# A state-space scan on one core: zero products on TensorE, a later sum, one more C buffer and |x| in place

## The chip, the core and the metric

The kernel runs on one core of a Trainium2 chip, in one launch. A core has five engines that run their own instruction queues in order: TensorE (matrix products, PE in the profile, with its weight loads as PEld), VectorE (DVE), ScalarE (ACT), GpSimd (POOL) and SyncE (SP), which here only issues DMAs. They meet through semaphores. TensorE writes to PSUM; the other operands lie in SBUF. The metric is device microseconds (us) of one execution: before the change 568.95, 570.45 and 570.57, so a median of 570.45 us.

## The reference, cut to what matters

Two layers run one after the other on a 64 x 64 image of 96 channels, all in float32. The change touches only the second, a Mamba layer over the sequence of L = 4096 pixels, with 192 inner channels and 16 states:

```
xs, z = split(gn(x) @ W_in.T);  xc = silu(causal_conv3(xs))
dt, B, C = split(xc @ W_x.T);   delta = softplus(dt @ W_dt.T + b_dt)
h[t] = exp(delta[t] * A) * h[t-1] + delta[t] * B[t] * xc[t]     # for each channel and state
y[t] = sum over states of h[t] * C[t]  + xc[t] * D
out = x + (y * silu(z)) @ W_out.T
```

## The kernel before, in words

**Tiles.** The sequence is cut into four chunks of 1024 steps (`NSC`, `CH`). The 192 channels are one full tile of 128 partitions and a half tile of 64. In a chunk the scan has 24 *units* (`UNITS`, `UNIT`): units 0 to 15 are one state each of the full tile, units 16 to 23 are two states each of the half tile, one state on either half of the partitions. So 96 units follow each other; s counts them, and `c, i = divmod(s, 24)` gives the chunk and the place in it. Data of the half tile are 512 columns wide per half (the columns `CH:CW` of a tile of `CW` = 1536), and are spread to the form of units 16 to 23 by DMAs (`front_dup`).

**One unit.** `load` (L1492) brings C[t] of the state, the same row on all partitions, by DMA from DRAM into a buffer of the pool `"C"`, which has six; `decay` (L1502) makes exp(delta*A) on ScalarE; `spread` (L1511) puts B[t] on all partitions of a PSUM tile `f` by two bf16 products (f has two buffers); `scan` (L1525) multiplies f by w = delta*xc on VectorE and runs the recurrence there into `h` (three buffers); `times_c` (L1544) multiplies the C buffer by h on GpSimd; `fold` (L1560) adds that product to the sum over states with two float32 matrix products, into `y0` (two banks, units 0 to 15) or `y1` (one bank, units 16 to 23). At i = 0 `fold` first calls `skip` (L1548), which starts the sum with xc*D. In five units of a chunk (`POOL_UNITS`, L42) B comes by DMA too, GpSimd multiplies it by w (`pool_f`), and the decay lies in an f buffer instead.

**The order.** Everything goes through the class `Ordered`, whose helper at L377 records each instruction and makes it follow the one before it on its engine; so nearly all rows of the profile have line L377, and the order is the order of the calls in `run` (L1804). Its loop does for each s, in this order: the next step of the *work between* (`all_between`); `load(s+3)`; `spread(s+1)` if that unit isn't one of GpSimd's; `keep_last(s-1)` (ScalarE saves the last column of h); the decays of the units ahead, and `pool_f`; the next step of `soft`; `scan(s)`; `times_c(s-1)`; `fold(s-2)`; and at i = 20 `gate(c, 0)` (L1579), where VectorE multiplies the finished y0 by silu(z).

**The work between** (`between`, L1738) prepares the next chunk and finishes the last one on TensorE and ScalarE, a step per unit, with at most two calls of a product in it, all through one PSUM bank `misc`. Names of its products in the profile: pc (convolution), pd (projection to dt, B, C), pv (delta before the softplus), pz (z), po (the output), pt (transposes of it). In chunks 1 and 2 the steps i = 2 and 3 are pd; at i = 4 VectorE gates y1 of the chunk before (`gate(c - 1, 1)`), and TensorE then starts the new y1 with `skip(c, 2)` and goes on to pv. In chunk 3 there is no pd, and this gate with its `skip` comes at i = 3, followed by po. In chunk 1 the last pc is copied by ScalarE at i = 14, and po follows in the same step; in chunk 2, po is copied at i = 12 before pt.

**The softplus** (`soft`, L1770) of the next chunk is spread over the units as well: from i = 15 in chunk 0 and from i = 10 in the others, one step per unit: |x| on ScalarE into a tile `e`; two sigmoids of e into `acc` and `q`; the first square of q; the second; `soft_times` on VectorE; the last VectorE operation, into dt; w = dt*u on GpSimd; the DMAs. In the opening chunk a part of it runs at i = 2 and after.

**What the steps of the prediction touch:** the functions named above, and the PSUM and SBUF buffers that make one engine wait for another: f (released by the scan), C (released by the fold, so SyncE's loads wait for TensorE), h (released by `times_c`, so a scan waits for GpSimd's third product before it), `misc` (released by a ScalarE copy).

Of the kernel before, what the change touches and what calls it, by code (L numbers as in the profile page):

```python
# [20 lines left out]
C = 96  # L21
DI = 192
NS = 16
# [14 lines left out]
UNIT = len(UNITS[0]) + len(UNITS[1])  # L38

WHOLE = 4  # L40

POOL_UNITS = ((5, 11, 15, 19, 23), (4, 8, 12, 16, 21), (4, 8, 12, 16, 21), (4, 8, 12, 16, 20))  # L42
CW = CH + NB
# [171 lines left out]
def soft_scalar(nc, k, e, last, q):  # L215

    soft_logistic(nc, k, e, last, q)
    for i in range(2):
        soft_square(nc, k, q, i)
# [1050 lines left out]
class Layer1:  # L1270
# [6 lines left out]
    def __init__(self, nc, tc, st, k, lay, w_in, conv_w, x1, stats, bc_dram, out, g):  # L1277
        self.k, self.lay, self.x1, self.bc_dram, self.out = k, lay, x1, bc_dram, out
        self.g = g
        self.pools = {  # L1280
            n: st.enter_context(tc.tile_pool(name=f"{n}_1{g}", bufs=b))
            for n, b in (
                ("fix", 1), ("xn", 2), ("uz", 2), ("sp", 1), ("dt", 2), ("dup", 2), ("dbl", 1),
                ("parts", 2), ("split", 1), ("B", 1), ("C", 6), ("dA", 3), ("h", 3), ("v", 1), ("oc", 1),
                ("ob", 2),
            )
        }
        fix = self.pools["fix"]
        self.cw = tap_weights(nc, fix, w_in, conv_w, 3, f"1{g}")
        self.nc = nc = Ordered(nc, tc)  # L1290
        with tc.tile_pool(name=f"gn1{g}", bufs=1, space=PSUM) as ps:

            warm = ps.tile([P, NB], F32, name=f"warm{g}")

            def busy(n, cols=NB):
                for _ in range(n):
                    nc.tensor.matmul(
                        warm[:, 0:cols], k["ident"][0:C, :], x1[:, 0:cols], start=True, stop=True
                    )

            busy(2)
            self.mean, self.rstd = group_norm_scale(
                nc, fix, ps, k["grp"], stats, f"1{g}", lambda: busy(1, NB // 2)
            )
            busy(2)
        self.shift = fix.tile([C, 1], F32, name=f"shift1{g}")
        nc.vector.scalar_tensor_tensor(
            self.shift, self.mean, -1.0, self.rstd, ALU.mult, ALU.mult
        )

        self.diag = fix.tile([P, 2, P], F32, name=f"diag{g}")
        for t in range(2):
            nc.gpsimd.tensor_scalar(
                self.diag[:, t, :], k["ident"], lay["vec"][:, DSK + t : DSK + t + 1], None, ALU.mult
            )
        self.last = fix.tile([P, UNIT], F32, name=f"last{g}")
        for n, b in (("f", 2), ("y0", 1), ("y1", 1), ("misc", 1)):
            self.pools[n] = st.enter_context(
                tc.tile_pool(name=f"{n}_1{g}", bufs=b, space=PSUM)
            )  # L1320
# [105 lines left out]
    def front_v(self, c):  # L1426
        nc, of = self.nc, self.chunks[c]
        self.at = c
        of["e"], of["dt"] = e, dt = self.tile("sp", [P, CW], "e"), self.tile("dt", [P, CW], "dt")
        of["acc"], of["q"] = self.tile("sp", [P, CW], "acc"), self.tile("sp", [P, CW], "q")  # L1430
        for q in range(3):
            ps = self.misc(c, [P, NB], f"pv{q}")
            yield from self.steps(self.product(ps, q, self.dt_taps(of["dbl"])))
            nc.scalar.activation(dt[:, self.part(q)], ps, AF.Identity, bias=self.vec(DTB, q))
# [141 lines left out]
                )  # L1576


    def gate(self, c, t):  # L1579
        of, col = self.chunks[c], (slice(0, CH), slice(CH, CW))[t]  # L1580
        self.at = c
        if t == 0:
            of["v"] = self.tile("v", [P, CW], "v")
        self.nc.vector.tensor_mul(of["v"][:, col], of[f"y{t}"], of["sz"][:, col])
# [70 lines left out]
    def start(self):  # L1655

        nc, of = self.nc, self.chunks[0]
        self.at = 0
        xn = of["xn"] = self.tile("xn", [C, CH + 2], "xn")
        nc.gpsimd.memset(xn[:, 0:2], 0.0)  # L1660
        nc.vector.tensor_scalar(
            xn[:, 2 : 2 + NB], self.x1[:, 0:NB], self.mean, self.rstd, ALU.subtract, ALU.mult
        )
        nc.scalar.activation(
            xn[:, 2 + NB :], self.x1[:, NB:CH], AF.Identity, scale=self.rstd, bias=self.shift
        )

        table = lambda func: nc.scalar.activation(self.k["root"], self.k["ones"], func)
        table(AF.Silu)
        self.front_xn(1)  # L1670
        self.at = 0
        u = of["u"] = self.tile("uz", [P, CW], "u")
        dbl = of["dbl"] = self.tile("dbl", [ROWS, CH], "dbl")
        e, acc, sq = of["e"], of["acc"], of["q"] = [
            self.tile("sp", [P, CW], n) for n in ("e", "acc", "q")
        ]
        dt = of["dt"] = self.tile("dt", [P, CW], "dt")

        def do(matmuls):
            for args, kw in matmuls:  # L1680
                nc.tensor.matmul(*args, **kw)

        def bank(pool, shape, name):
            self.at = name
            return self.tile(pool, shape, pool)

        pc = [bank("f", [P, NB], f"pc{p}") for p in range(2)] + [self.misc(0, [P, NB], "pc2")]
        pd = [bank(f"y{hf}", [ROWS, NB], f"pd{hf}") for hf in range(2)]

        for p in range(3):  # L1690
            do(self.product(pc[p], p, self.conv_taps(xn)))
            nc.scalar.activation(u[:, self.part(p)], pc[p], AF.Silu, bias=self.vec(CB, p))
        table(AF.Sigmoid)
        for hf in range(2):
            do(self.project(0, hf, pd[hf]))
            nc.vector.tensor_copy(dbl[:, self.part(hf)], pd[hf])
            self.write_bc(0, hf)
        pv = [bank("f", [P, NB], f"pv{p}") for p in range(2)] + [self.misc(0, [P, NB], "pv2")]
        for p in range(3):
            do(self.product(pv[p], p, self.dt_taps(dbl)))  # L1700
        for p in range(2):
            col = self.part(p)
            nc.scalar.activation(e[:, col], pv[p], AF.Abs, bias=self.vec(DTB, p))
            soft_scalar(nc, self.k, e[:, col], acc[:, col], sq[:, col])
            nc.vector.tensor_scalar(dt[:, col], pv[p], self.vec(DTB, p), 0.0, ALU.add, ALU.max)
        for s in range(3):
            self.load(s)
        for p in range(2):
            col = self.part(p)
            soft_vector(nc, dt[:, col], acc[:, col], sq[:, col])  # L1710
        self.front_w(0, (slice(0, CH),), nc.vector)
        self.spread(0)
        self.spread(1)

        pz, pz1 = bank("y0", [P, 2, NB], "pz"), bank("y1", [P, NB], "pz1")
        for q in range(2):
            do(self.product(pz[:, q], q, self.z_taps(xn)))
        do(self.product(pz1, 2, self.z_taps(xn)))
        for s in range(2):
            self.decay(s)  # L1720
        nc.scalar.activation(dt[:, self.part(2)], pv[2], AF.Identity, bias=self.vec(DTB, 2))
        for _ in self.front_b(0, halves=True):
            pass
        self.at = 0
        sz = of["sz"] = self.tile("uz", [P, CW], "sz")
        for q in range(3):
            nc.scalar.copy(sz[:, self.part(q)], pz[:, q] if q < 2 else pz1)
# [42 lines left out]
    def soft(self, c):  # L1770

        def piece(c, col):

            nc, k = self.nc, self.k
            e, dt, acc, q = (self.chunks[c][n][:, col] for n in ("e", "dt", "acc", "q"))
            nc.scalar.activation(e, dt, AF.Abs)
            yield
            soft_logistic(nc, k, e, acc, q)
            yield
            for i in range(2):  # L1780
                soft_square(nc, k, q, i)
                yield
            soft_times(nc, acc, q)
            yield
            nc.vector.scalar_tensor_tensor(dt, dt, 0.0, acc, ALU.max, ALU.add)
            yield
            self.front_w(c, (col,), nc.gpsimd)
            yield
            self.front_dup(c)
            yield  # L1790
# [13 lines left out]
    def run(self):  # L1804
# [2 lines left out]
        self.units = [{} for _ in range(n)]  # L1807
        self.start()
        work, end = self.all_between(), self.end()
        for s in range(n + 2):  # L1810
            c, i = divmod(s, UNIT)
            if i == 0 and c < NSC:
                soft = self.soft(c)
# [19 lines left out]
                self.times_c(s - 1)  # L1833
            if s == n:
                next(end)
            if s >= 2:
                self.fold(s - 2)
            if i == NS + 4 and c < NSC:
                self.gate(c, 0)
        for _ in end:  # L1840
# [9 lines left out]
def tile_kernel(  # L1850
# [38 lines left out]
    k["within"] = const.tile([P, DIRS, WIN], F32, name="within")  # L1889
    nc.gpsimd.memset(k["within"], 1.0)  # L1890
    nc.gpsimd.memset(k["within"][:, :, 0:1], 0.0)

    lay0, lay1 = {}, {}

# [116 lines left out]
```

## Time and profile before

| | |
|---|---|
| runs | 568.95, 570.45, 570.57 us; median 570.45 |
| profiled execution | 571.18 us, of which the span from first to last instruction is 569.4 |
| busy: TensorE | 482.6 us (85%), 1363 products |
| busy: VectorE | 461.7 us (81%), 442 instructions |
| busy: ScalarE | 328.4 us (58%) |
| busy: GpSimd | 348.8 us (61%) |
| mean granted TensorE clock | 0.899 |
| first scan of layer 1 starts, last ends | 188.9 us, 554.1 us |

Shares over the whole span mix the two layers. The part that the change touches is the stretch of the 96 units, from about 189 to 554 us. There the rows to read are those of VectorE, and what ended each of its idle times. A row of the timeline gives start, length, engine, line, operation, `out<-in`, shapes and how often, and in brackets the idle time before it with what ended it. In the list of waits the numbers are total us, how often, and the longest.

### The profile page before, as it was taken

What the parts mean: (1) busy time and instruction counts of PE and PEld (TensorE: products, weight loads), DVE (VectorE), ACT (ScalarE), POOL (GpSimd) and SP (SyncE); (2) the same over time, 40 slices, a digit from 0 to 9 for tenths busy, and PEclk for the clock granted to TensorE, in tenths of its full rate; (3) what the DMA queues carried; (4) which work ended last, traced back from release to release, by engine and by line L of the source; (5) the groups of instructions that cost most, each with busy time, mean ns of one, the idle gap of its engine ahead of it and who ended that gap; (6) DMA issues with size and microseconds to landing.
All of it is one profiled execution on the core that took longest, in us unless ns stands there. A gap on an engine that the chain in (4) does not pass through costs nothing.

```text
span 569.4 us, 4766 instructions
## 1 busy us (share of the span) xinstructions
PE 482.6 (85%) x1363; PEld 195.3 (34%) x1363; DVE 461.7 (81%) x442; ACT 328.4 (58%) x486; POOL 348.8 (61%) x204
## 2 busy tenths in 40 slices
PE   4999999988889998996899978679976847986782
PEld 3545445436732333331133323113422202432220
DVE  6897989255733979998989979896978899899991
ACT  5437993478636876695856765464585454243300
POOL 7080010014320697989997859975886988789861
PEclk9996999997997999997599979779989767999778
DMA  6103800000003537786655649764648675677701
GB/s 170 21 9 72 281 2 0 0 1 1 2 28 113 155 130 222 214 202 154 192 195 188 207 94 224 201 187 126 199 142 198 149 184 184 199 238 190 191 22 35
DMA packets 30502, 75.76 MB, mean 133 GB/s; under 512 B 10880, under 2 KB 12156, under 8 KB 30210
## 3 DMA queue, kind: packets, MB, share of 16 engines
q1 hardware_dynamic: 29186, 73.83, 45.8%
q10 hardware_dynamic: 1280, 1.52, 0.9%
q8 instruction: 13, 0.21, 0.2%
q14 instruction: 23, 0.19, 0.1%
HBM read 68.93 MB, written 2.25 MB: 125 GB/s over the span
## 4 chain that ended last, share of the span: by engine, by line
PE 24%; DVE 23%; ACT 11%; POOL 5%; issue 4%; DMA 4%; SPq 1%; POOLq 0%; DVEq 0%; ACTq 0%
DVE h L377 15%; PE y L377 11%; DVE f L377 5%; PE f L377 3%; ACT q L377 3%; POOL C L377 2%; PE pd L377 2%; ACT dA L377 2%; PE po L377 2%; DMA C<-bc_dram 2%; ACT f L377 2%; SPq L377 1%; PE pc L377 1%; ACT L377 1%; PE pv L377 1%
## 5 line engine op out<-in xcount | busy, mean ns | idle before, releaser
L377 POOL TENSOR_TENSOR C<-C,h 128x1024 f32<-128x1024 f32 x96 | 229.5, 2403 | 51.4 <-issue 19.6
L377 DVE TENSOR_TENSOR_SCAN h<-dA,last,f 128x1024 f32<-128x1024 f32 x57 | 133.8, 2347 | 7.9 <-POOL C L377 0.5
L377 PE MATMUL y<-C,ident 128*128 128x512 f32 x256 | 130.5, 632 | 4.5 <-POOL C L377 4.3
L377 DVE TENSOR_TENSOR f<-f,w 128x1024 f32<-128x1024 f32 x76 | 92.4, 1215 | 16.8 <-PE f L377 16.2
L377 ACT ACTIVATE dA<-dt,A 128x1024 f32<-128x1024 f32 x76 | 86.3, 1143 | 2.2 <-DVE h L377 1.9
L377 PE MATMUL f<-parts,pick 96*128 96x512 bf16 x144 | 50.5, 437 | 35.6 <-DVE h L377 35.6
L377 PEld LDWEIGHTS y<-C,ident 128*128 128x128 f32 x256 | 50.9, 203 | 60.5 <-issue 43.1
L377 PE MATMUL pc<-pad,cw 96*128 96x512 f32 (+1 forms) x144 | 59.8, 576 | 0.8 <-ACT v L377 0.8
L377 PE MATMUL y<-C,both 128*64 128x512 f32 x128 | 44.2, 784 | 9.8 <-POOL C L377 9.8
L377 POOL TENSOR_TENSOR B<-B,w 128x1024 f32<-128x1024 f32 x20 | 47.1, 2354 | 7.2 <-DMA B<-bc_dram 7.2
L377 ACT COPY last<-h 128x1 f32<-128x1 f32 x72 | 13.5, 187 | 64.2 <-DVE h L377 64.1
L377 DVE TENSOR_TENSOR_SCAN h<-dA,f 128x1024 f32<-128x1024 f32 x19 | 43.4, 2287 | 2.4 <-POOL C L377 0.2
L377 PEld LDWEIGHTS <-pick 96*128 96x128 bf16 x144 | 10.9, 102 | 94.1 <-DVE h L377 47.1
L377 ACT ACTIVATE f<-dt,A 128x1024 f32<-128x1024 f32 x20 | 22.3, 1116 | 35.3 <-DVE h L377 26.9
L377 PEld LDWEIGHTS pc<-pad,cw 96*128 96x128 f32 x144 | 28.5, 200 | 32.0 <-issue 27.7
L377 ACT ACT_TABLE_LOAD x28 | 35.9, 1283 | 2.1 <-PEq L2001 1.7
L377 DVE TENSOR_TENSOR_SCAN h<-f,last,B 128x1024 f32<-128x1024 f32 x15 | 34.9, 2330 | 0.0
L377 PE MATMUL pc<-xn,cw 96*64 96x512 f32 (+1 forms) x84 | 29.9, 603 | 0.1
L377 POOL TENSOR_SCALAR ln_small<-ln_small 128x4 f32<-128x4 f32 x2 | 0.5, 235 | 42.5 <-DVE ln_small L377 42.5
L377 POOL TENSOR_TENSOR rest<-dbl,parts 96x1024 f32<-96x1024 f32 (+1 forms) x5 | 10.0, 2000 | 26.0 <-ACT parts L377 25.8
L377 POOL MEMSET wda<- 128x4 f32 (+3 forms) x8 | 0.9, 119 | 37.3 <-ACT wda L377 37.3
L377 PEld LDWEIGHTS y<-C,both 128*64 128x64 f32 x128 | 7.8, 161 | 31.7 <-POOL C L377 20.7
(212 smaller groups left out, 727.9 us busy)
## 6 DMA issues: line engine op xcount, KB each, us to landing
C<-bc_dram SPq DMA_DIRECT2D x64, 512.0 KB, 4.0
C<-bc_dram SPq DMA_DIRECT2D x64, 256.0 KB, 4.7
B<-bc_dram SPq DMA_DIRECT2D x12, 512.0 KB, 5.4
B<-bc_dram SPq DMA_DIRECT2D x16, 256.0 KB, 5.4
dt<-dt SPq DMA_DIRECT2D x16, 128.0 KB, 4.4
w<-w SPq DMA_DIRECT2D x16, 128.0 KB, 4.0
wB<-rows_dram SPq DMA_DIRECT2D x1, 1472.0 KB
wC<-rows_dram SPq DMA_DIRECT2D x1, 1472.0 KB
```

Source lines behind the costliest of these rows:

```text
L377: ins = it(*args, **kw)
```

## The change

Five edits, all but one in layer 1:

1. `LAG = 3`: `fold` is called for unit s - 3 instead of s - 2, and the loop runs one step longer. The pool C has `4 + LAG` = 7 buffers instead of 6.
2. `hold(s)`, called right after `fold`: products of a zero 128 x 128 matrix with 512 columns of ones, added to y0 or y1. One call at i = 4 and i = 20 of each chunk; in chunk 0 two more at i = 19 and two more at i = 20; in chunks 1 and 2 two at i = 14 and two at i = 15. That is 20 calls.
3. Softplus: |x| goes into `q` and the second sigmoid runs in place, so the tile `e` is gone.
4. Softplus: both squares are issued in the step of the first one; the step of the second is left empty.
5. The zero matrix is a new constant, set by GpSimd at the start of the program.

```diff
+LAG = 3
-  ("parts", 2), ("split", 1), ("B", 1), ("C", 6), ("dA", 3), ...
+  ("parts", 2), ("split", 1), ("B", 1), ("C", 4 + LAG), ("dA", 3), ...
+    def hold(self, s):
+        c, i = divmod(s, UNIT)
+        n = 1 if i in (4, 20) else 0
+        if c < NSC - 1 and i in ((19, 20) if c == 0 else (14, 15)):
+            n += 2
+        of = self.chunks[c]
+        for _ in range(n):
+            self.nc.tensor.matmul(
+                of["y0"][:, 0:NB] if i < NS else of["y1"], self.k["zero"],
+                free(self.k["within"], (1, NB)), start=False, stop=False,
+            )
...
-            nc.scalar.activation(e, dt, AF.Abs)
+            nc.scalar.activation(q, dt, AF.Abs)
             yield
-            soft_logistic(nc, k, e, acc, q)
+            soft_logistic(nc, k, q, acc, q)
             yield
             for i in range(2):
                 soft_square(nc, k, q, i)
-                yield
+            yield
+            yield
             soft_times(nc, acc, q)
...
-        for s in range(n + 2):
+        for s in range(n + LAG):
...
-            if s >= 2:
-                self.fold(s - 2)
+            if s >= LAG:
+                self.fold(s - LAG)
+            if s < n:
+                self.hold(s)
...
+    k["zero"] = const.tile([P, P], F32, name="zeros")
+    nc.gpsimd.memset(k["zero"], 0.0)
```

More of the change, by code (lines that the diff above doesn't have):

```diff
@@ L1283, in __init__ @@
                 ("fix", 1), ("xn", 2), ("uz", 2), ("sp", 1), ("dt", 2), ("dup", 2), ("dbl", 1),
-                ("parts", 2), ("split", 1), ("B", 1), ("C", 6), ("dA", 3), ("h", 3), ("v", 1), ("oc", 1),
+                ("parts", 2), ("split", 1), ("B", 1), ("C", 4 + LAG), ("dA", 3), ("h", 3), ("v", 1), ("oc", 1),
                 ("ob", 2),
@@ L1428, in front_v @@
         self.at = c
-        of["e"], of["dt"] = e, dt = self.tile("sp", [P, CW], "e"), self.tile("dt", [P, CW], "dt")
+        of["dt"] = dt = self.tile("dt", [P, CW], "dt")
         of["acc"], of["q"] = self.tile("sp", [P, CW], "acc"), self.tile("sp", [P, CW], "q")
@@ L1673, in start @@
         dbl = of["dbl"] = self.tile("dbl", [ROWS, CH], "dbl")
-        e, acc, sq = of["e"], of["acc"], of["q"] = [
-            self.tile("sp", [P, CW], n) for n in ("e", "acc", "q")
-        ]
+        acc, sq = of["acc"], of["q"] = [self.tile("sp", [P, CW], n) for n in ("acc", "q")]
         dt = of["dt"] = self.tile("dt", [P, CW], "dt")
@@ L1702, in start @@
             col = self.part(p)
-            nc.scalar.activation(e[:, col], pv[p], AF.Abs, bias=self.vec(DTB, p))
-            soft_scalar(nc, self.k, e[:, col], acc[:, col], sq[:, col])
+            nc.scalar.activation(sq[:, col], pv[p], AF.Abs, bias=self.vec(DTB, p))
+            soft_scalar(nc, self.k, sq[:, col], acc[:, col], sq[:, col])
             nc.vector.tensor_scalar(dt[:, col], pv[p], self.vec(DTB, p), 0.0, ALU.add, ALU.max)
@@ L1774, in piece @@
             nc, k = self.nc, self.k
-            e, dt, acc, q = (self.chunks[c][n][:, col] for n in ("e", "dt", "acc", "q"))
-            nc.scalar.activation(e, dt, AF.Abs)
+            dt, acc, q = (self.chunks[c][n][:, col] for n in ("dt", "acc", "q"))
+            nc.scalar.activation(q, dt, AF.Abs)
             yield
-            soft_logistic(nc, k, e, acc, q)
+            soft_logistic(nc, k, q, acc, q)
             yield
```

## The prediction, on record before the result

> **What bounds the kernel now.** I read first the rows of the page by engine, then VectorE's waits inside the 96 units, then the timelines around each wait. VectorE's work there is the floor: 76 units of a multiply and a scan (1.21 + 2.35 us, with their gaps some 3.6), 20 units of a scan alone (2.3), four softpluses, seven gates. Between 188.9 and 554.1 us it stands still for only 27 us, in 19 places. VectorE's own waits between 190 and 570 us (total, times, longest):
>
> ```profile
> DVE f L377 <- PE f L377: 16.2, 12, 3.9
> DVE acc L377 <- ACT q L377: 9.6, 4, 3.8
> DVE h L377 <- POOL C L377: 0.7, 2, 0.5
> DVE h L377 <- ACT f L377: 0.5, 1, 0.5
> ```
>
> So 16.2 us are a spread of B that TensorE delivers late, 9.6 a softplus whose second square isn't done. The sum can fall by 27 us at the very most. The timeline of TensorE in chunk 1 shows both its clock and its queue (start, length, x records):
>
> ```profile
> 329.66 1.15 ACT L377 ACTIVATE dA<-dt,A 128x1024 f32<-128x1024 f32 x1
> 330.71 1.56 ACT L377 ACTIVATE q<-q,soft 128x1536 f32<-128x1536 f32 x1
> 332.17 0.67 ACT L377 ACTIVATE u<-pc,vec 128x512 f32<-128x512 f32 x1
> ...
> 332.30 2.56 DVE L377 SCALAR_TENSOR_TENSOR acc<-q,acc 128x1536 f32<-128x1536 f32 x1 [3.85 <-ACT q L377]
> ...
> 332.89 2.02 PE L377 MATMUL po<-x,ident 96*96 96x512 f32 x2 [3.46 <-ACT u L377]
> 334.70 1.92 PE L377 MATMUL po<-v,w_out 128*96 128x512 f32 x2
> 336.41 1.06 PE L377 MATMUL f<-parts,pick 96*128 96x512 bf16 x2
> 337.26 2.53 PE L377 MATMUL y<-C,ident 128*128 128x512 f32 x4
> 339.73 1.09 PE L377 MATMUL po<-v,w_out 64*96 64x512 f32 x2
> 340.75 1.98 PE L377 MATMUL y<-C,ident 128*128 128x512 f32 x4
> 342.57 0.49 PE L377 MATMUL pt<-ident,oc 96*128 96x96 f32 x4
> 343.75 0.60 PE L377 MATMUL f<-parts,pick 96*128 96x512 bf16 x2 [0.68 <-DVE h L377]
> 345.91 1.02 PE L377 MATMUL po<-x,ident 96*96 96x512 f32 x2
> ```
>
> A float32 call is two records: 1.8 us from start to start at 332.89, when the clock is low, and 0.86 at full clock (345.91 to the next start at 346.77). And after ScalarE's copy at 332.17 TensorE has no pause until 343.07: only 0.68 us of room.
>
> The third kind, late in chunks 1 and 2: the sum waits for GpSimd, and the spread queued behind it is late.
>
> ```profile
> 365.29 1.97 PE L377 MATMUL y<-C,both 128*64 128x512 f32 x4 [3.44 <-POOL C L377]
> ...
> 368.90 0.78 PE L377 MATMUL f<-parts,pick 96*128 96x512 bf16 x2
> ...
> 369.72 1.23 DVE L377 TENSOR_TENSOR f<-f,w 128x1024 f32<-128x1024 f32 x1 [1.68 <-PE f L377]
> ```
>
> **Edits with no price of their own.** The zero constant: a 128x128 MEMSET on GpSimd is 0.20 us, put before the 3.72 us MEMSET of `pad` at 3.36, long before that tile is read. |x| in place: the same five ScalarE instructions, in order anyway. The 7th C buffer: load(s+3) used to wait for the sum of s-3, now for s-4, both issued at step s-1; SyncE's queue, with the softplus's DMAs and `out` behind the loads, is moved no further back, and POOL's queue is untouched. The end: three last sums instead of two after the y_end products; the last waits for GpSimd's product (it ends at 556.6) as before, and the one more 1.08 us sum fits between 553.6 and there: 0.
>
> **The later sum** takes one fold out from before each spread, which gives only where folds differ or wait. **The 20 zero calls** cost TensorE 20 x 0.86 = 17.2 us; each costs nothing where TensorE then waits for VectorE, and all of it where it doesn't; it waits for nothing of its own. **The squares:** step i's second square no longer stands behind the next step's decays. I go place by place, in times of the old timeline; a minus is a gain.
>
> A, opening (199 to 212). The sum of unit 0 waits for GpSimd until 199.55 and its four calls stand before the spread at 202.23; a step later they don't: -1.05, and ScalarE's u and decay behind it: -0.49. The second square (0.7) now precedes the decay (1.14): -1.07. The zero call at i = 4 ends by about 207, the next spread is wanted at 209. Sum -2.6; I take **-2.5** (0, if GpSimd's C products, late until 204, hold the scans; -2.8 with the 0.21 that it holds at 199.5).
>
> B, softplus in chunk 0. The first square ends 253.2; the second then ends 254.7, before the scan ends at 256.2: -2.61. Behind it the decays end at about 258, wanted at 258.7. What is late next is GpSimd: rest can't start before ScalarE's cast (259.7, unmoved), then two C products, w 3.4, B 2.35, parts 2.1: scan 24 needs the third product before it, at 278.3, while VectorE could be there at 277.9: +0.4. The zero calls (1.72 and 2.6 us) fall into TensorE's 4.21 us wait before 263.53. **-2.2** (-0.5, if rest, w and B each take as long as rest beside VectorE, 3.45; -2.6 if GpSimd keeps up).
>
> C, start of chunk 1. The spread at 297.76 stands behind two pd, both y0 sums with `skip` and one sum more; now a half-tile sum (1.08) takes the place of a full one (1.72), and skipped waits give back the rest: the 1.61 us wait becomes about 0.5 with the zero call of i = 4 (0.86) counted; and 0.35 us slack used up at 302 comes back as a wait at 315. **-0.6** (+0.8 to -1.5).
>
> D, softplus in chunk 1. On ScalarE the second square moves before the decay (1.15): acc starts at 331.1, -1.15. But the copy u still ends at 332.8, so TensorE's chain above is unmoved, and four zero calls (3.44 us) now stand in it: 343.1 + 3.4, the spread of unit 41 ends at 347.0, where VectorE wants it at 344.7: +2.3, and +0.3 at the next one. Further on, the waits of 0.60 and 1.68 go since no sum waits; GpSimd's C product is next late: +0.3. Sum **-0.5** (+3.3 if the calls run at the low clock, 1.8 each; -3.4 if they hide).
>
> E, start of chunk 2. TensorE runs from 377.09 to 411 without a pause, at low clock until 386.4. One fold less (1.8) before the spread of unit 53, one zero call more (0.86): the 0.77 stays, 3.90 becomes 2.9 + 0.45 behind, and slack is gone by unit 57. **-0.4** (+1.2 if the clock rises one window later, to -1.5).
>
> [...]
>
> F, softplus in chunk 2. The 2.56 us wait at 424.48 stays: the spread stands behind pt, which waits for ScalarE's copy oc behind the sigmoids. The square: 2.02 becomes 0.45, -1.57. The waits of 1.14, 0.49 and 0.65 come from sums waiting for GpSimd: -2.28. The zero calls meet TensorE's 4.28 us wait before 441.18, but ob is copied 1.5 us later and pushes them: +0.7. **-3.1** (-1 to -4).
>
> G, start of chunk 3. Here the later sum hurts. Before, the first y0 sums with `skip` (3.44 us) ran at 478.8, while TensorE waited for the gate of 481.46. Now the last y1 sum runs there, TensorE idles until 482.1, and those 3.44 us follow `skip` and po, in front of unit 77's spread: at full clock that spread is ready at 489.9 (no change), at low clock until 485 at 491.4, until 488 at 493. I take **+1.5** (0 to +3.1).
>
> **Sum:** -2.5 - 2.2 - 0.6 - 0.5 - 0.4 - 3.1 + 1.5 = -7.8 us. The profiled execution took 571.18: 563.4. It stands 0.7 above the median of the runs, so the forecast is **562.7 us**.
>
> **Rivals.**
> 1. *The zero calls hide.* If TensorE has more room at D than I read (the trace lacks some records), D is -3.4 and C, E and F are each 0.5 better: 12.2 us, so 558.3. For it: after 443 and 357 TensorE waits for VectorE. Against: 0.68 us of room at D. Chance 0.15.
> 2. *GpSimd takes over.* It works some 290 of the 365 us, and a scan waits for its third product before; the h waits at 199.5 and 464.0 show it already at the limit. Should it give back half of A, B and F (3.9), 4 us are left: 566.5. Against: it has gaps over 5 us (333 and 394). Chance 0.2.
> 3. *Slower: the zero calls stand in front.* Without them the edits give about 12.5 us; all 20 in front of a wanted spread cost 17.2, so 575.2; it decides from 15 of the 20 calls on, or 7 at low clock (1.8 each). For it: D, and spreads at 231.5, 297.8, 311 and 394.8 that are just in time. Against: the pauses at B and F. Chance 0.13.
> 4. *It does nothing:* ScalarE's and TensorE's chains replace each wait by an equal one, as 2.56 at F. 570.4; chance 0.07.
>
> My forecast has 0.45.
>
> **How the numbers follow.** A measurement of this kernel tells about 0.3% (1.7 us) from no change. Forecast, 1 and 2 are faster: 0.8, less a little for their poor ends: 0.78. Within 0.3%: 0.08; slower: 0.14. The range reaches from rival 1 past rival 2 to the poor ends of D and E with half of C's (3.8 + 1.6 + 0.9 more): **557.5 to 569.0**; rivals 3 and 4 lie outside. The forecast's own range is 560 to 566.
>
> **What would show it.** Right: no wait of acc at 253 to 259, some 2.7 left in chunk 1 and 0.5 in chunk 2; sums of y that no longer wait for C; f waits of about 2.3 us at unit 41 and 3.4 at unit 77; 20 new calls, at 0.86 us. Wrong: f waits at 41 absent (rival 1), h waiting for C for more than 2 us in all (rival 2), f waits behind zero calls at i = 4 (rival 3). The forecast fails worst if the clock behaves otherwise at E and G.

## The result, and the profile after

| | before | after |
|---|---|---|
| median of 14 runs each | 569.12 us (565.71 to 572.29) | 577.23 us (572.39 to 579.92) |
| profiled execution | 571.18 us | 576.95 us |
| mean granted TensorE clock in it | 0.899 | 0.906 |
| first scan of layer 1 to the end of the last | 365.2 us | 371.8 us |
| busy: VectorE | 461.7 us | 468.1 us, in the same 442 instructions |

The ratio of the times is 1.0132, with an interval of 1.0101 to 1.0164: the change makes the kernel slower by 1.3%, where 562.7 us and a gain of 1.4% were forecast. In the two profiled executions the 96 units are 6.6 us apart. Over all profiles here the first scan starts between 187.7 and 191.7 us, ahead of the work that the edits move, so a profile is read by its 96 units and not by its end. Executions of one kernel differ by some 2% (the kernel before took 561.76 to 573.12 us in 35 runs on one chip); a ratio is formed from undisturbed ones alone, so it can stand elsewhere than that of the medians of all runs.

VectorE's waits after the change, in the window of the units (total us, how often, the longest):

```profile
DVE f L379 <- PE f L379: 18.7, 15, 5.3
DVE acc L379 <- ACT q L379: 3.9, 2, 3.0
DVE h L379 <- POOL C L379: 2.5, 3, 1.1
DVE h L379 <- POOL B L379: 1.4, 2, 1.1
```

The waits for ScalarE fell from 9.6 to 3.9 us, as the early squares were to do. What TensorE delivers late rose from 16.2 to 18.7, and GpSimd's share from 0.7 to 3.9. The sum is where it was, near 27 us. So waits alone don't account for 6.6 us: VectorE's own rows became longer. Its groups by shape (count, then busy us and mean ns of one, then idle time before them), after and then before:

```profile
L379 DVE SCALAR_TENSOR_TENSOR dt<-dt,acc 128x1536 f32<-128x1536 f32 x3 | 10.7, 3553 | 0.0
L379 DVE SCALAR_TENSOR_TENSOR acc<-q,acc 128x1536 f32<-128x1536 f32 x3 | 8.4, 2798 | 3.9 <-ACT q L379 3.9
```

```profile
L377 DVE SCALAR_TENSOR_TENSOR acc<-q,acc 128x1536 f32<-128x1536 f32 x3 | 7.1, 2361 | 8.5 <-ACT q L377 8.5
L377 DVE SCALAR_TENSOR_TENSOR dt<-dt,acc 128x1536 f32<-128x1536 f32 x3 | 5.2, 1732 | 0.0
```

The same six instructions took 12.3 us before and 19.1 after. One of them grew most, in chunk 0. VectorE and GpSimd there, in the timeline after the change:

```profile
255.47 1.73 DVE L379 SCALAR_TENSOR_TENSOR acc<-q,acc 128x1536 f32<-128x1536 f32 x1
255.69 3.74 POOL L379 TENSOR_TENSOR C<-C,h 128x1024 f32<-128x1024 f32 x1 [0.41 <-issue]
259.44 2.13 POOL L379 TENSOR_TENSOR rest<-dbl,parts 96x1024 f32<-96x1024 f32 x1
259.65 5.84 DVE L379 SCALAR_TENSOR_TENSOR dt<-dt,acc 128x1536 f32<-128x1536 f32 x1
261.53 2.34 POOL L379 TENSOR_TENSOR C<-C,h 128x1024 f32<-128x1024 f32 x1
265.57 3.42 POOL L379 TENSOR_TENSOR w<-dt,u 128x1536 f32<-128x1536 f32 x1 [1.70 <-DVE dt L379]
```

The same place before:

```profile
258.83 2.45 DVE L377 SCALAR_TENSOR_TENSOR acc<-q,acc 128x1536 f32<-128x1536 f32 x1 [2.61 <-ACT q L377]
259.81 3.45 POOL L377 TENSOR_TENSOR rest<-dbl,parts 96x1024 f32<-96x1024 f32 x1
263.40 1.73 DVE L377 SCALAR_TENSOR_TENSOR dt<-dt,acc 128x1536 f32<-128x1536 f32 x1
263.61 3.73 POOL L377 TENSOR_TENSOR C<-C,h 128x1024 f32<-128x1024 f32 x1 [0.35 <-DVE h L377]
```

In these rows whichever starts second is longer by about the rest of the first. Before, VectorE's dt came 0.21 us ahead of GpSimd's product: dt 1.73, the product 3.73 instead of its usual 2.35. After, GpSimd's `rest` came 0.21 us ahead of dt, and dt didn't even get its turn behind it: it took 5.84, which is 1.92 to the end of `rest`, 2.3 for the whole product queued behind `rest`, and 1.6 of its own. The time that dt stood blocked is counted nowhere as idle: the row shows it as busy.

The second large place is the start of chunk 3, where the later sum was expected to hurt. TensorE and VectorE after the change:

```profile
481.01 1.98 PE L379 MATMUL y<-C,both 128*64 128x512 f32 x4
484.23 2.08 PE L379 MATMUL y<-u,diag 128*128 128x512 f32 x2 [1.24 <-DVE v L379]
486.09 1.91 PE L379 MATMUL po<-x,ident 96*96 96x512 f32 x2
487.80 1.92 PE L379 MATMUL po<-v,w_out 128*96 128x512 f32 x2
...
494.67 0.61 PE L379 MATMUL f<-parts,pick 96*128 96x512 bf16 x2
```

```profile
483.50 0.67 DVE L379 TENSOR_TENSOR v<-y,sz 128x512 f32<-128x512 f32 x1
495.32 1.23 DVE L379 TENSOR_TENSOR f<-f,w 128x1024 f32<-128x1024 f32 x1 [5.28 <-PE f L379]
```

The products from 484.23 to 489.51 take up to twice their time (1.9 for two records, against 1.02 at 490.97). The 1.24 us of idle time didn't lower the clock; it had long been low: the granted clock is 1.00 until 460, within the 3.68 us that TensorE stands idle before 460.90, and then 0.50 in every 2 us until 490, the last 6 us of it unbroken work; it is 0.82 from 490 to 492 and 1.00 from 492 to 494. The spread of unit 77 is 5.28 us late, where it was 1.88.

### The profile page after: what moved, and what is told of

The parts are those of the page before. It is cut to its first block, busy times and chain, and to the rows that moved or that the text cites. A ratio compares the mean times of both kernels' runs of the same rounds, so it can differ in the third digit from the quotient of the medians.

```text
span 575.2 us, 4845 instructions
## 1 busy us (share of the span) xinstructions
PE 497.2 (86%) x1403; PEld 200.3 (35%) x1403; DVE 468.1 (81%) x442; ACT 329.4 (57%) x486; POOL 348.0 (60%) x205
## 4 chain that ended last, share of the span: by engine, by line
PE 26%; DVE 25%; ACT 11%; issue 4%; POOL 4%; DMA 3%; DVEq 0%; POOLq 0%; SPq 0%; ACTq 0%
DVE h L379 16%; PE y L379 12%; DVE f L379 6%; ACT q L379 3%; PE po L379 3%; PE pd L379 3%; PE f L379 3%; ACT dA L379 2%; ACT f L379 2%; POOL C L379 2%; DVE dt L379 1%; ACT L379 1%; PE pv L379 1%; PE pc L379 1%; ACT acc L379 1%
## 5 line engine op out<-in xcount | busy, mean ns | idle before, releaser
L379 PE MATMUL y<-C,ident 128*128 128x512 f32 x256 | 127.9, 623 | 0.0
L379 DVE TENSOR_TENSOR f<-f,w 128x1024 f32<-128x1024 f32 x76 | 92.3, 1215 | 19.0 <-PE f L379 18.7
L379 PE MATMUL y<-C,both 128*64 128x512 f32 x128 | 45.9, 814 | 4.3 <-POOL C L379 4.3
L379 PEld LDWEIGHTS <-pick 96*128 96x128 bf16 x144 | 11.3, 102 | 84.8 <-DVE h L379 45.9
L379 POOL TENSOR_TENSOR rest<-dbl,parts 96x1024 f32<-96x1024 f32 (+1 forms) x5 | 8.7, 1743 | 26.1 <-ACT parts L379 26.0
L379 ACT ACTIVATE q<-q,soft 128x512 f32<-128x512 f32 (+1 forms) x18 | 20.6, 1146 | 0.5
```

Of the source, the lines that this page charges most:

```text
L379: ins = it(*args, **kw)
```

## The experiments

All start from the kernel before or after, keep its whole computation, and have |x| in place and the zero constant. There were three theories. *GpSimd* (P in the expectations): the early squares move VectorE's two softplus operations onto GpSimd's products. *TensorE*: the zero products (Z) or the later sum (L) stand in front of spreads. Each ratio is to the kernel before on the same chip, with its 95% interval, and the medians of all runs stand beside it; two kernels whose intervals overlap are not ranked by time alone.

| kernel | median, us | before, us | ratio |
|---|---|---|---|
| squares only | 571.22 | 568.03 | 1.0048 (1.0004 to 1.0093) |
| later sum only | 570.24 | 568.03 | 1.0024 (0.9984 to 1.0064) |
| zero products only | 571.94 | 568.03 | 1.0052 (1.0014 to 1.009) |
| after, `rest` behind the product | 572.48 | 568.03 | 1.0046 (1.0001 to 1.009) |
| after, no zero products | 571.34 | 569.37 | 0.9958 (0.991 to 1.0007) |
| `rest` behind, softplus a unit later | 571.30 | 569.37 | 1.0055 (1.0021 to 1.0089) |
| after, sums catch up at unit 72 | 571.08 | 569.37 | 0.9956 (0.9891 to 1.0021) |
| `rest` behind, later softplus, catch-up, no zero products | 568.10 | 569.37 | 0.9952 (0.9907 to 0.9996) |
| `rest` behind, catch-up, no zero products (the three repairs) | 565.54 | 568.77 | 0.9947 (0.991 to 0.9984) |
| the three repairs, squares as before | 563.40 | 568.77 | 0.9925 (0.9891 to 0.996) |
| the three repairs, zero products at the turns | 568.54 | 568.77 | 1.0003 (0.9971 to 1.0034) |
| the three repairs, GpSimd's unit 16 at 17 | 562.10 | 568.77 | 0.9902 (0.9865 to 0.9939) |

In two rows (after without zero products; after with the catch-up) the ratio lies below 1 and the median 0.3% above the other. Neither is taken as a gain over before.

**The early squares alone.**

```diff
             for i in range(2):
                 soft_square(nc, k, q, i)
-                yield
+            yield
+            yield
```

> The kernel before with both squares in one step and |x| in place; sums two units behind, no zero products. [...] Theory Z (the zero products cost the time) and theory L (the later sum costs all of it): nothing here costs anything, 4 to 5 us shorter.

Measured: 1.0048, so 2.7 us above before by the ratio, where GpSimd's theory had the two operations 2 to 6 us longer and the time at most 1 us above, and the other two had 4 to 5 us below. The wait for ScalarE is gone in chunk 0 and short in chunk 2, but the operations behind it are longer. For each softplus, the wait before acc and the lengths of acc and dt, added (us, from the timelines of VectorE):

| | chunk 0 | chunk 1 | chunk 2 |
|---|---|---|---|
| before | 2.61+2.45+1.73 = 6.79 | 3.85+2.56+1.73 = 8.14 | 2.02+2.08+1.73 = 5.83 |
| later sum only | 2.76+1.76+1.73 = 6.25 | 3.99+2.41+1.73 = 8.13 | 2.22+1.90+1.73 = 5.85 |
| squares only | 0+2.10+1.73 = 3.83 | 3.00+3.41+1.73 = 8.14 | 0.68+3.41+2.75 = 6.84 |
| after | 0+1.73+5.84 = 7.57 | 3.00+3.42+1.73 = 8.15 | 0.86+3.24+3.08 = 7.18 |
| after, no zero products | 0+1.83+5.91 = 7.74 | 3.00+3.41+1.73 = 8.14 | 0.86+3.24+2.81 = 6.91 |
| after, `rest` behind the product | 0+1.73+1.73 = 3.46 | 3.00+3.41+1.73 = 8.14 | 0.42+3.68+2.83 = 6.93 |
| three repairs, GpSimd's unit at 17 | 0+1.92+1.73 = 3.65 | 3.00+1.76+1.73 = 6.49 | 0.86+3.24+1.73 = 5.83 |

This table carries the case. In chunk 1 the sum is 8.13 to 8.15 us whether the square is early or late, until the last row moves GpSimd's product away. In the rows acc starts inside that product and ends after it (before, then after):

```profile
330.90 2.34 POOL L377 TENSOR_TENSOR B<-B,w 128x1024 f32<-128x1024 f32 x1
332.30 2.56 DVE L377 SCALAR_TENSOR_TENSOR acc<-q,acc 128x1536 f32<-128x1536 f32 x1 [3.85 <-ACT q L377]
...
334.46 2.34 POOL L379 TENSOR_TENSOR B<-B,w 128x1024 f32<-128x1024 f32 x1
335.01 3.42 DVE L379 SCALAR_TENSOR_TENSOR acc<-q,acc 128x1536 f32<-128x1536 f32 x1 [3.00 <-ACT q L379]
```

In both, acc ends 1.6 us after the multiply of B. In chunk 2 the early squares cost about 1.0. Only in chunk 0 do they give (3 us), and there only if GpSimd's order lets dt through. By this table the three softpluses gain 1.95 us in the kernel with the squares alone, and its 96 units took 364.9 us against 365.2. Its one profile doesn't show where the 0.5% of its times comes from: the units there begin 2.8 us later than before, by work that the edit doesn't touch.

**The later sum alone**: `LAG = 3` and seven C buffers, no call of `hold`, squares as before.

> The kernel before with sums three units behind, the seventh C buffer and |x| in place; squares apart, no zero products. P: spreads no longer stand behind sums that wait for GpSimd (some 6 us less waiting in the opening and late in chunks 1 and 2), against some 3 us more at the start of chunk 3 and 2 to 4 at the start of chunk 1: within 2 us of before. L: 5 us or more above before. Z: about 5 us below before.

Measured: 1.0024, within 2 us of before, as GpSimd's theory had it. The gains forecast for a sum that no longer waits came: the waits of 0.60 and 1.68 late in chunk 1 went, and 1.14 and 0.65 in chunk 2 (aligned with before scan by scan, -0.7, -1.8, -1.2 and -0.8). They were given back at three places: 1.7 at unit 12 (the kernel after has the same wait of 1.73; there TensorE is idle for 2.37 us before 216.99, the granted clock is 0.50 from 218 to 220 and 0.73 to 222, a sum of four records takes 3.39 us instead of 1.88, and TensorE has no pause until that unit's spread at 230.83); 6.68 in place of 3.90 at unit 53; 4.49 in place of 1.88 at unit 77. TensorE's rows ahead of unit 53:

```profile
376.23 4.04 PE L379 MATMUL pd<-u,w_x 128*118 128x512 f32 x4
...
383.07 4.04 PE L379 MATMUL pd<-u,w_x 128*118 128x512 f32 x4
...
393.86 0.61 PE L379 MATMUL f<-parts,pick 96*128 96x512 bf16 x2
```

**The zero products alone**: the kernel before with the 20 products of `hold`.

> The kernel before with the 20 zero products and |x| in place; sums two units behind, squares apart. P: 0 to 2 us above before, since VectorE's waits behind them in the trace after are 0.2 to 0.5 us each. Z: 5 us or more above before. L: no change, or a gain of 1 to 2 us from the higher clock.

Measured: 1.0052, 3.0 us above before, between the 0 to 2 of GpSimd's theory and the 5 or more of the zero products'. Spreads are later than before at chunk 1's start (unit 29 waits 2.86, +1.25), at units 41 and 47 (1.41, +1.41, and 2.36, +0.68) and at unit 77 (2.84, +0.96). But the same pd, at the same place as above:

```profile
386.22 2.16 PE L379 MATMUL pd<-u,w_x 128*118 128x512 f32 x4
388.32 0.60 PE L379 MATMUL f<-parts,pick 96*128 96x512 bf16 x2
392.19 2.07 PE L379 MATMUL pd<-u,w_x 128*118 128x512 f32 x4
398.24 0.61 PE L379 MATMUL f<-parts,pick 96*128 96x512 bf16 x2
```

Here both pd run at full clock, by their lengths (before, 2.07 us goes with a granted clock of 1.00 and 4.04 with 0.50), and unit 53 waits 0.61 us instead of 3.90 before. Over all the profiles this wait follows the lengths of the two pd: 6.6 and 6.7 us with both at 4.04; 3.5 to 4.1 with the first alone at 4.04; 1.6 to 2.3 with the first at 2.5 to 3.3. No zero product stands between unit 20 of chunk 1 and these pd. So the zero products don't hold the clock up for them; that the clock's steps fall elsewhere in a run whose earlier work has other times is argued, not shown. It is one likely source of the scatter of 2%.

Taken one by one, the three parts stand 0.5, 0.2 and 0.5% above before, where the 0.2 isn't clear of zero; together they cost 1.3%. No part alone is a gain.

**GpSimd's `rest` behind the product** (after, chunk 0):

```diff
-            if i in ((18, 20, 21, 22) if c == 0 else (14, 16, 18, 20)):
+            if c == 0 and i == 20:
+                self.late = parts
+            elif i in ((18, 21, 22) if c == 0 else (14, 16, 18, 20)):
                 next(parts, None)
...
                 self.times_c(s - 1)
+            if s == 20:
+                next(self.late)
```

> The kernel after, with one exchange on GpSimd in step 20 of chunk 0: the subtraction into rest comes after the C product of that step instead of before it. Nothing else is moved. P: at that step VectorE's last softplus operation (dt, 5.84 us after, 1.73 before) then starts just ahead of GpSimd's C product, takes 1.7 us, and the C product some 3.7; the time falls by 2 to 4 us against the kernel after. [...]

Measured: 572.48 us, 1.0046. The distance to before is 4.45 us by the medians where it was 8.1, and 0.46% where it was 1.32%: 3.7 to 4.9 us of the loss went; 2 to 4 were expected if GpSimd's products hold dt, at most 1 if they don't. GpSimd and VectorE in chunk 0:

```profile
255.74 3.74 POOL L379 TENSOR_TENSOR C<-C,h 128x1024 f32<-128x1024 f32 x1 [0.22 <-issue]
259.93 3.73 POOL L379 TENSOR_TENSOR C<-C,h 128x1024 f32<-128x1024 f32 x1 [0.45 <-DVE h L379]
263.62 2.13 POOL L379 TENSOR_TENSOR rest<-dbl,parts 96x1024 f32<-96x1024 f32 x1
```

```profile
255.53 1.73 DVE L379 SCALAR_TENSOR_TENSOR acc<-q,acc 128x1536 f32<-128x1536 f32 x1
259.71 1.73 DVE L379 SCALAR_TENSOR_TENSOR dt<-dt,acc 128x1536 f32<-128x1536 f32 x1
```

Nothing was taken out; two GpSimd instructions changed places. dt now starts 0.22 us before the product, runs its 1.73, and it is the product that takes 3.73. That shows the cause of the 5.84. The row shrank by 4.1 us, and the time by about as much, though the intervals of the two ratios all but touch.

**After without the zero products.**

```diff
-            if s < n:
-                self.hold(s)
```

> The kernel after without the 20 zero products; all else as after. Alone they cost 0.5% of the kernel before. [...] Z (the zero products are most of the loss): 6 us or more below the kernel after, level with before.

Measured: 571.34 against 569.37 us, about +0.3%, the ratio's interval reaching 1.0007. By the medians that is 6 us less than after, level with before: the time that the theory of the zero products had. The rows are as GpSimd's theory had them: dt in chunk 0 stayed at 5.91 and the wait at unit 77 at 4.77. The waits for spreads fell from 18.7 to 11.5 us, but 3.0 of these 7.2 lie at unit 29, where both pd ran at full clock this time; they did so too in the kernel with `rest` behind the product, which has the zero products. So the zero products cost several us of the 8.1, how many is open, and taking them away doesn't bring the forecast gain.

**The softplus a unit later** (with `rest` behind): one more `yield` ahead of `soft_times`, so that no wait for the square is left.

> The kernel of the exchanged rest, with one more empty step ahead of VectorE's softplus operations, so that they come one unit later in every chunk. P: GpSimd's B product, which held VectorE's acc until 1.7 us after its start in chunks 1 and 2 (acc 3.4 and 3.7 us), is over by then, and the squares are long done: acc takes 1.7 to 2.1 us and no longer waits for a square; 3 to 5 us below the kernel of the exchanged rest. If instead TensorE's queue is what ends last there, VectorE's waits for f grow by as much and the time stays.

Measured: 571.30 us, 1.0055: none of the 3 to 5 us that were expected below the kernel that it starts from. acc waits nowhere and takes 1.73, 2.90 and 1.73 us. But in chunk 0 dt, a step later, takes 5.95 again; that other GpSimd products hold it there is the author's estimate, from the order of the calls. In chunks 1 and 2 the sums of the table above fall to 4.63 and 4.34, but TensorE's spreads are then the late ones (new waits of 1.70, 1.96 and 2.65). Moving VectorE's operations made acc shorter in chunks 1 and 2, and dt in chunk 0 long again.

**The sums catch up before chunk 3's turn** (after):

```diff
-        for s in range(n + LAG):
+        for s in range(n + 2):
...
+            if s == 72:
+                self.fold(69)
             if s >= LAG:
-                self.fold(s - LAG)
+                self.fold(s - (LAG if s < 72 else 2))
```

> The kernel after, but at the first unit of chunk 3 two sums are called, and from there they are two units behind again. P: the first sums of chunk 3 lie again before the gate and not in front of unit 77's spread: that wait falls from 5.3 us to the 1.9 of before; 2 to 4 us below the kernel after. If the wait there comes from the low clock alone, it stays above 4 us.

Measured: 571.08 against 569.37 us. The spread of unit 77 and what stands before it on TensorE:

```profile
477.37 1.13 PE L379 MATMUL y<-u,diag 128*128 128x512 f32 x2
478.33 1.02 PE L379 MATMUL po<-x,ident 96*96 96x512 f32 x2
479.19 1.02 PE L379 MATMUL po<-v,w_out 128*96 128x512 f32 x2
480.05 1.88 PE L379 MATMUL y<-C,ident 128*128 128x512 f32 x4
481.86 1.09 PE L379 MATMUL po<-v,w_out 64*96 64x512 f32 x2
482.89 0.61 PE L379 MATMUL f<-parts,pick 96*128 96x512 bf16 x2
```

With the y0 sums back ahead of the gate, TensorE doesn't stop, the products run at full clock by their lengths (1.02 us for two records, as after the change at 492.69, where the granted clock was 1.00), and the wait of 5.28 is 0.36. It is 0.36 in all six kernels with the catch-up; in the five with sums three behind and no catch-up it is 3.67 to 5.28, in the three with sums two behind 1.70 to 2.84. In this execution dt of chunk 0 was not held (1.73), with the order of the kernel after unchanged there: acc happened to take longer (2.43 instead of 1.73); that dt came ahead of `rest` by it is inferred from dt's length. The race of 0.2 us can go either way, so this kernel's time, 6.4 us below after by the medians, holds both and isn't the price of the catch-up alone.

**Repairs together.** First `rest` behind the product, the later softplus, the catch-up and no zero products:

> All mends together: exchanged rest, softplus operations one unit later, two sums at the first unit of chunk 3 and two units behind from there, no zero products. P: the waits for sums that wait for GpSimd (4 to 5 us), those for the squares (9.6 us) and the port (2 us) go, and the start of chunk 3 is as before: 8 to 14 us below before, some 556 to 561. If TensorE's queue takes the place of what goes, 3 us or less below before.

568.10 us, 0.9952: 1 to 3 us below before instead of 8 to 14, with both pd at 4.04 in the profiled execution (6.55 of wait at unit 53) and dt in chunk 0 at 5.92. Then the same without the later softplus:

> The kernel after with three mends: rest after the C product in step 20 of chunk 0, two sums at the first unit of chunk 3 and two units behind from there, no zero products. Softplus steps as after. P (now: port race in chunk 0, the later sum in chunk 3, zero products, each some 4 to 6 us by the runs so far): 3 to 7 us below before, 562 to 566; the wait at unit 77 below 1 us, dt in chunk 0 at 1.7. If the mends only move the waits to TensorE, level with before.

565.54 us, 0.9947: faster than before, with dt in chunk 0 at 1.73 and the wait at unit 77 at 0.36. The repairs don't add up: against after, by the medians and each with its own before, they brought 3.7, 6.1 and 6.4 us one by one and 11.3 together. Then the same with the squares as they were before the change:

```diff
             for i in range(2):
                 soft_square(nc, k, q, i)
-            yield
-            yield
+                yield
```

> The kernel with the three mends, but the two squares in two steps as before. P: in chunks 1 and 2 nothing changes, since there GpSimd's B product sets the end of acc and not the square (acc starts 0.8 to 1.2 us later and is as much shorter); only chunk 0 loses, some 2 to 3 us. If the squares set the end in all chunks: 4 us or more above the kernel with the three mends.

563.40 us, 0.9925, where a loss of 2 to 3 us was expected. The intervals overlap, so late squares are not shown to be better; but early ones give nothing that can be measured even in the mended kernel: 2.2 us in chunk 0 (4.06 against 6.25, summed as in the table), of which chunk 2 takes 1.3 back (7.11 against 5.84).

**Zero products at the turns**: ten of them at i = 23, 0 and 1 around the starts of chunks 1 and 2, to hold the clock for the pd.

> The kernel with the three mends and ten zero products in other places: one at i = 23 and two each at i = 0 and 1 of the turns to chunks 1 and 2, where TensorE waits for VectorE and the clock falls before pd. Clock theory: both pd of chunk 2 run at 2.2 us instead of up to 4.0, the wait at unit 53 falls to 2 us or less (it was 1.6 to 6.7 in the runs so far, by the lengths of pd), 1 to 4 us below the kernel with the three mends and less scatter. If zero products do not hold the clock up, or what stands behind them is late: level or above.

568.54 us, 1.0003. Both pd of chunk 2 took 2.07 and 2.16, so by their lengths the clock was up there; unit 53 still waited 1.59, as without them (2.56 and 2.16), and new waits of 1.40 and 2.63 stood at the start of chunk 1. So the full clock for the pd, which the theory had right, brought no time: 1 to 4 us were expected below the kernel of 565.54 us.

**GpSimd's own unit moved** from i = 16 to 17 in chunks 1 and 2, in the kernel of 565.54 us:

```diff
-POOL_UNITS = (..., (4, 8, 12, 16, 21), (4, 8, 12, 16, 21), ...)
+POOL_UNITS = (..., (4, 8, 12, 17, 21), (4, 8, 12, 17, 21), ...)
```

> The kernel with the three mends, with GpSimd's unit 16 in chunks 1 and 2 moved to unit 17, so that its B product comes one step later and no longer lies beside VectorE's acc. P: acc in chunks 1 and 2 takes 1.7 to 2 us instead of 3.3 to 3.7, its wait for the square stays (3.0 and 0.4 to 0.9); 1 to 3 us below the kernel with the three mends. [...]

562.10 us, 0.9902 (0.9865 to 0.9939): the lowest median, and faster than the kernels before and after. VectorE's rows in chunks 1 and 2:

```profile
329.32 1.76 DVE L379 SCALAR_TENSOR_TENSOR acc<-q,acc 128x1536 f32<-128x1536 f32 x1 [3.00 <-ACT q L379]
334.59 1.73 DVE L379 SCALAR_TENSOR_TENSOR dt<-dt,acc 128x1536 f32<-128x1536 f32 x1
421.32 3.24 DVE L379 SCALAR_TENSOR_TENSOR acc<-q,acc 128x1536 f32<-128x1536 f32 x1 [0.86 <-ACT q L379]
428.27 1.73 DVE L379 SCALAR_TENSOR_TENSOR dt<-dt,acc 128x1536 f32<-128x1536 f32 x1
```

Moving GpSimd's multiply of B away took 1.64 us out of acc in chunk 1 (3.40 to 1.76) and 1.3 out of dt in chunk 2 (3.02 to 1.73); acc in chunk 2, which was expected at 1.7 to 2, stays at 3.24, its length in the kernel after, where it starts beside a product with C (429.25 to 431.61) and ends 1.61 us behind it. In exchange scans wait 3.9 us for C in all. How much this last edit gives beyond the kernel it starts from is open: the intervals overlap, and the 96 units took 355.3 and 355.0 us in the two profiles.

## Why the prediction was wrong, point by point

The two profiled executions, aligned scan by scan, give for each of the prediction's places (us, minus is a gain):

| place | predicted | measured | what it was |
|---|---|---|---|
| A, opening | -2.5 | -2.3, then +1.0 | the waits went; dt 0.67 became 1.64 |
| unit 12, not foreseen | 0 | +1.7 | a spread late behind sums at low clock |
| B, softplus, chunk 0 | -2.2 | +0.9 | -3.1, then dt +4.1 |
| C, start of chunk 1 | -0.6 | +3.4 | first pd at low clock: 4.04 us, 2.16 before |
| D, softplus, chunk 1 | -0.5 | -0.9 | acc's wait -0.85, its length +0.86; later, fewer waits behind sums |
| E, start of chunk 2 | -0.4 | -1.7 | first pd 3.25 us, 4.04 before |
| F, softplus, chunk 2 | -3.1 | +1.0 | wait -1.16, acc +1.16, dt +1.35 |
| G, start of chunk 3 | +1.5 | +3.4 | low clock for longer than taken |
| sum | -7.8 | +6.5 | |

**The step that failed most is the price of the softplus operations, in B, D and F.** The prediction wrote "the second then ends 254.7, before the scan ends at 256.2: -2.61" and "2.02 becomes 0.45, -1.57": it took the waits for the square as the time to be had, and the lengths of acc and dt as VectorE's own, though for GpSimd's side it knew the collision ("as long as rest beside VectorE, 3.45"). The profile of before already said otherwise: acc at 332.30 took 2.56 us where dt, of the same shape, took 1.73, and 332.30 lies inside GpSimd's multiply of B (330.90, 2.34 us). acc ends about 1.6 us after GpSimd's multiply does, square early or late. Ending a wait earlier only lengthens the row behind it: -0.85 and +0.86 in D, -1.16 and +1.16 in F. In B there was a real gain of 3.1, and dt's race with `rest` then cost 4.1. Of the 14.3 us between forecast and measurement this step holds about 7.0: 0.9 + 2.2 in B, 1.35 + 1.57 in F, and 1.0 for the opening's dt. In the opening the early square wasn't what gained either: the later sum alone gives the same steps there (-1.15, +0.63, -1.75, +0.97), and with the squares alone acc takes 2.24 us where it waited 1.07 and took 1.27 before.

The rows of the two engines agree in one thing: acc goes from 1.73 to between 3.2 and 3.7 us where GpSimd's instruction is first, and GpSimd's products with C from 2.35 to 3.73 where acc or dt is; VectorE's scans and its multiplies by w keep to means of 2.27 to 2.35 and of 1.21 us before and after. What in the chip makes the one instruction wait for the other isn't shown. The expectations of two runs call it a port and set 2 us and 4 to 6 us to it; no run shows a port. What the runs showed in its place are longer rows, 19.1 us for the six softplus operations after against 12.3 before, and some 4.1 us back, by the rows, where `rest` was put behind the product.

**C and G failed in the clock.** C's first pd was priced at the full clock of the old timeline; it ran at 4.04 us, since the clock fell in the 2.01 us of idle time before 283.12 (a mean of 0.88 granted from 281 to 283, then 0.50 until 291), which no term held. Of all 14 profiles only this one has a pd of chunk 1 at low clock, and with the zero products and the later sum both in, the wait at unit 29 was 0.55 and 0.76 in two others instead of 3.51: how much of C belongs to the change and how much to this execution stays open. G had the right place and sign ("Here the later sum hurts"), and its poor end of +3.1, low clock until 488, fell just short of the measured +3.4: the clock was low until 490.7, some 488.7 in times of before, and the value in the middle was mis-sized. The catch-up shows that G's loss is the moved sums: it goes when they stay in front of the gate. E came out better than forecast because its first pd ran at 3.25 us instead of 4.04; that is luck, as this pd takes anything from 2.07 to 4.05 over the profiles. Its poor end of +1.2, in the range too, was for a clock that rises a window later; no run shows such a window, only this pd's lengths and waits at unit 53 of 0.61 to 6.68. The prediction said that it would fail worst by the clock at E and G; these two miss by -1.3 and +1.9, less than the softplus and C.

**D's zero calls** were priced at +2.3 before unit 41, and the wait there was 0.18. Both ends of that sum had moved: acc ended no earlier, so VectorE asked later, and the sum before the spread took 1.88 us instead of 2.53. That D as a whole came out near its forecast is luck: neither the gain of 1.15 nor this loss came. At other places spreads were later with them: in the kernel with them alone, at units 29, 41, 47 and 77.

**The later sum** did what was written: the waits of 0.60, 1.68, 1.14 and 0.65 behind sums that waited for GpSimd went in the kernel with it alone, and in the whole change they were partly replaced by scans waiting for GpSimd (3.9 us in all, 2.5 of them for C: the sign of rival 2, "for more than 2 us in all").

**The rivals.** Rival 3's time, 575.2, is nearest, but its mechanism, all twenty zero products in front of spreads, is a part only: they cost 3.0 us alone and some 6 within the change, not 17.2, and without them the kernel still doesn't beat the one before. It is near by luck. Rival 2 named the right engine, and priced it by waits for GpSimd's results, not by VectorE's rows that GpSimd makes longer; it had 566.5. Its "some 290" us of GpSimd's work are 305 in the profile. One more slip changes nothing: half of C's way from -0.6 to +0.8 is 0.7, where the range's upper end adds 0.9.

## What to carry to other kernels

A VectorE or GpSimd row that is longer than another of its shape can be a wait in disguise (here 5.84 us for 1.73 and 3.74 for 2.35): before pricing an earlier start, take the same instruction's shortest row, and look what the other engine runs beside each longer one. Where two engines hold each other up like that, an order that a few tenths of a us decide can be worth more than the work moved: here 0.21 us decided between 1.73 and 5.84 us for dt, and two exchanged GpSimd instructions gave back about half the loss. A shorter row alone is no gain either: moving one GpSimd unit by a step took 1.64 us out of a VectorE row, and the 96 units took as long in its profile as without that move. Time saved on a wait is only a gain where the end of what follows is free to move; the sum of wait and length, compared over kernels, tells that in one line.

## What was not expected of the hardware

- dt took 5.84, 5.91, 5.92 and 5.95 us for 1.73 in four kernels. In the first, the kernel after, the rows show two GpSimd instructions in a row beside it: the second starts at 261.53, as the first ends, and dt ends 1.62 us behind the second.
- The granted clock at one place of the program differs between nearly equal programs: the two pd at the start of chunk 2 took 4.04 and 4.04 us or 2.16 and 2.07, which sets 6 us of wait. It fell within idle times of 1.99 us (before, a mean of 0.78 granted from 375 to 377) and 2.01 us (after, 0.88 from 281 to 283); it then stayed at 0.50 through some 9.3 and 9.7 us of unbroken work.
